# Attention over kept tokens: in the last pair of heads the short chunk goes second, and the output chunks are finished and stored one by one

## The chip, the cores and the metric

The kernel runs on one core of one Trainium2 chip. The metric is device time in microseconds (us). Before the change the median of three runs was 635.94 us (634.38 to 639.89).

## The reference

```
def _L0_cond_ref(x, mask, Wq, Wo):        # x (8, 512, 1024), mask (8, 1024) of 0 and 1
    NH = 8; NEG = -1e+30
    B, D, T = x.shape
    dk = D // NH                          # 64
    scale = 1.0 / sqrt(dk)
    xt = transpose(x, (0, 2, 1))
    q = xt @ Wq.T
    qh = q.reshape(B, T, NH, dk).transpose(0, 2, 1, 3)
    scores = scale * einsum('bhqd,bhkd->bhqk', qh, qh)
    logits = (scores * cmask + (1.0 - cmask) * NEG) * rmask
    attn = softmax(logits, axis=-1)
    ctx = einsum('bhqk,bhkd->bhqd', attn, qh)
    out = ctx.transpose(0, 2, 1, 3).reshape(B, T, D) @ Wo.T
    return transpose(out, (0, 2, 1))
x = x + _L0_cond_ref(x, cond_2048, Wq, Wo)
```

Queries, keys and values are the same projection. The mask (`cmask` over keys, `rmask` over queries) is 1 for about half of the 1024 tokens. A token whose mask is 0 gets the mean over all tokens; the kept tokens attend to kept tokens only.

## The kernel before

The kernel works on the kept tokens alone. For each batch it gathers them into a compact list of NK = 536 places (KH = 268 is half of it), so that the list falls into five chunks of keys and of output rows: four long ones of 128 (`c` or `i` = 0 to 3) and a short one of 24 (`LAST` = 4). Everything is float32. The eight heads of a batch are taken as four pairs (`pr` = 0 to 3), `pairs` lists (batch, pair) in order, and `late` runs over them. There is no scheduler: each engine executes in the order in which the code is written, and `plan` is a table, written by hand, that puts side work (projections, transposes, output products, loads) into slots named (batch, pair, chunk).

In the slot of chunk `c` of a pair:

- `scores(pair, c)`: TensorE (PE) multiplies the queries of the pair with the keys of the chunk into PSUM tiles of tag "s" (two tiles of two banks each; a long chunk uses both, one per head, the short one uses one). ScalarE (ACT) then takes the exponential into `e` (or `el` for the short chunk), one instruction per head, and adds up the sums for the softmax.
- `open_slot` notes what PE has to wait for before it writes with another row tile: the first reader of a "t" bank in the last slot, or else the exponential of head 0 of this slot. `pass_gate` hangs that wait on the first product of `weigh`.
- `weigh_behind(pair, before, c)`: PE multiplies values with `e` of chunks whose exponentials are done (`weigh`, into the two banks `av`). A long chunk is weighed in two halves (`cross` 0 and 1), the short one once.

After a pair, `end_values` copies `av` to `cT`, and `inverses` turns the sums into reciprocals. `spread` sends these through PE (`rb`) to all rows; `contexts` multiplies them into `cT`. For the last pair of all `end_values_last` multiplies `av` with `rb` on VectorE (DVE), first half, then `sum_last`, then second half.

The output of a batch is the product of `cT` of its four pairs with `woT`, one bank of 128 rows by 512 for each long chunk. In the last batch it is made in two steps. `begin_output` adds pairs 0 to 2 in a "t" bank, and ACT copies that to a tile `pa` (tag "xin"). `end_output` multiplies pair 3 in a bank `po`, DVE adds `pa` and writes `oc`, and SP stores `oc` to the DRAM tensor `od`. `plan` puts `begin_output` of the short chunk and of chunks 0 and 1 into slot 3 of the last pair, that of chunk 2 into slot 4; that of chunk 3 stands in `late` behind the last pair.

Then `fetch_last` issues eight indirect DMAs from GpSimd (POOL), which gather for each 128 tokens their rows of `od` into tiles `g`; the first reads the short chunk and chunk 0, the second also chunk 1, the third also chunk 2, the others all. `finish_tokens` transposes each `g` on PE (`o`), adds x on DVE and writes the result from ACT's queue.

Of the kernel before, what the change touches and what calls it, by code (L numbers as in the profile page):

```python
# [10 lines left out]
F32 = mybir.dt.float32  # L11
# [294 lines left out]
def attention_of_kept_tokens(ctx, tc, x, mask, wq, wo, out, ident, wqT, woT, verdict, flag):  # L306
# [360 lines left out]
    def open_slot():  # L667

        gate[0] = reader[0] or reader[1]
        reader[0] = None  # L670
# [52 lines left out]
    def weigh(pair, c, cross):  # L723


        v, e = vs[pair], es[pair, c]
        first = (pair, c) not in begun
        begun.add((pair, c))
        if c == 0 and first:
            avs[pair] = [bank("av_%d_%d_%d" % (*pair, hf), "av") for hf in range(2)]  # L730
        for r in range(2):
            rows = slice(r * DK, (r + 1) * DK)
            hf = r ^ cross
            for h in range(2):
                mm = nc.tensor.matmul(  # L735
                    avs[pair][hf][heads[h], :KH],
                    v[rows, c, heads[h]],
                    e[rows, h, hf, :] if c < LAST else e[rows, h, :],
                    start=(c == 0 and first),
                    stop=(c == LAST),  # L740
                )
                pass_gate(mm)

    def weigh_behind(pair, before, c):


        cross = c in (2, 4)
        if c == 0:
            if before:
                weigh(before, LAST - 1, cross)  # L750
                weigh(before, LAST, cross)
            return
        if c > 1:
            weigh(pair, c - 2, cross)
        weigh(pair, c - 1, cross)
# [16 lines left out]
    def end_values_last(pair):  # L772

        cT = place_contexts(pair)
        for hf, av in enumerate(avs.pop(pair)):
            if hf:
                sum_last(pair)
            cols = slice(hf * KH, (hf + 1) * KH)
            nc.vector.tensor_tensor(cT[:, cols], av[:, :KH], rbs[pair][:, cols], ALU.mult)
        mean_last(pair)  # L780
# [200 lines left out]
    def plain(pr):  # L981
        return woT[:, pr, :].rearrange("p (a d f) -> p d a f", a=A, d=ND)

    def last_products(b, i, prs, po):

        n = max(Q, sizes[i])
        for pr in prs:
            first, last = pr == prs[0], pr == prs[-1]
            if i < LAST:
                to = po.rearrange("p (d a f) -> p d a f", a=A, d=ND)  # L990
                nc.tensor.matmul(  # L991
                    to, cTs[b, pr][:, i * P : i * P + n], plain(pr), start=first, stop=last
                )
                continue
            w = D * n // P
            for j in range(P // n):
                nc.tensor.matmul(
                    po[j * n : (j + 1) * n, :w].rearrange("p (d a f) -> p d a f", a=A, f=Q),
                    cTs[b, pr][:, i * P : i * P + n],
                    plain(pr)[:, j * (w // P) : (j + 1) * (w // P)],  # L1000
                    start=first,
                    stop=last,
                )
# [4 lines left out]
    def begin_output(b, i):  # L1008

        po = bank(f"pa_{b}_{i}")  # L1010
        last_products(b, i, range(ND - 1), po)
        pa = sb.tile([P, D], F32, tag="xin", name=f"pa_{b}_{i}", bufs=NC)
        note(nc.scalar.copy(pa[:, : width(i)], po[:, : width(i)]))
        partials[i] = pa

    def end_output(b, i, tag):
        n, w = max(Q, sizes[i]), width(i)
# [316 lines left out]
    def plan():  # L1334
# [5 lines left out]
        def put(b, pr, c, task, *args, rank=0):  # L1340
            todo[b, pr, c].append((rank, task, args))
# [109 lines left out]
            for i, at in enumerate(ends):  # L1451
                put(*at, finish_blocks, b, i, rank=(2, 2, 2, 6.8, 4.5)[at[2]])

        last = B - 1
        for i in (LAST, 0, 1, 2):
            put(last, 3, 3 + (i == 2), begin_output, last, i, rank=7)
        for k in range(ND):
            put(*((0, 3, 1), (0, 3, 2), (0, 3, 3), (1, 1, 2))[k], mix_weights, k, rank=5.5)
        put(0, 0, 1, turn_mixed, rank=7)
# [9 lines left out]
    def late(n):  # L1469
# [41 lines left out]
        for p, pair in enumerate(pairs):  # L1511
            b, pr = pair
            before = pairs[p - 1] if p else None
            final = p + 1 == len(pairs)
            for c in range(NC):
                scores(pair, c)
                open_slot()
                tasks = sorted(todo[b, pr, c], key=lambda t: t[0])
# [26 lines left out]
        while stores[0] or stores[1]:  # L1545
            issue_stores()
        last = pairs[-1]
        open_slot()
        weigh_behind(None, last, 0)
        spread(last, inverses(last))  # L1550
        begin_output(B - 1, LAST - 1)
        end_values_last(last)
        worst = sb.tile([P, 2], F32, tag="worst", name="worst")
        nc.vector.tensor_reduce(
            worst[:, 0:1], low.rearrange("p h c -> p (h c)"), axis=AX.X, op=ALU.min
        )
        nc.vector.tensor_reduce(worst[:, 1:2], lowest, axis=AX.X, op=ALU.min)
        nc.vector.tensor_tensor(worst[:, 0:1], worst[:, 0:1], worst[:, 1:2], ALU.min)
        for j, i in enumerate((LAST, 0, 1, 2, 3)):
            end_output(B - 1, i, ("t", "av")[j % 2])  # L1560
            if i == LAST:
                pt = ps.tile([P, 2, NB], F32, tag="s", name="worst_t")
                nc.tensor.transpose(pt[:1, 0, :P], worst[:, 0:1], ident)
            elif i == 1:
                one = sb.tile([1, 1], F32, tag="one", name="one")
                nc.vector.tensor_reduce(one, pt[:1, 0, :P], axis=AX.X, op=ALU.min)
                nc.vector.tensor_scalar(one, one, TINY, None, ALU.is_lt)
        nc.vector.tensor_copy(flag, one)
        fetch_last(B - 1)
# [105 lines left out]
```

## Time and profile before

| what | value |
|---|---|
| profiled execution | 637.8 us, span from first to last instruction 635.8 us |
| median of three runs | 635.94 us (634.38 to 639.89) |
| PE busy | 591.4 us (93% of the span) |
| DVE, ACT, POOL busy | 404.7, 348.2, 253.1 us |
| chain that ended last | PE 74%, DMA 9%, DVE 6%, issue 4% |
| HBM | 181 GB/s over the span |

The chain is followed back from the last instruction, at each step to what released it. A name such as `pa L991` gives the tile that is written and the line. A row of the timeline merges like instructions: start, length, engine, line, operation, tiles, shape, count, and in brackets the idle time before it with what ended it. A float32 product on PE shows as two instructions. The profiled execution lay 1.9 us above the median; the work that the change touches lies in its last 55 us.

### The profile page before, as it was taken

How to read it: one execution, taken by the hardware profiler on the slowest of the kernel's cores; microseconds unless marked ns; L12 is line 12 of the kernel's file. 1: busy time of each engine (PE TensorE's matmuls, PEld its weight loads, DVE VectorE, ACT ScalarE, POOL GpSimd, SP SyncE). 2: the span in 40 equal slices, each digit the busy share in tenths (PEclk: the TensorE clock that was granted, in tenths of full speed). 3: DMA queues.
4: the chain of work that ended last, by engine and by line, in shares of the span. 5: the costliest groups of instructions: out<-in, count | busy, mean ns of one | idle time of the engine just before them, and what ended most of it. 6: DMA issues, size and time to landing. Idle time of an engine off the chain costs nothing.

```text
span 635.8 us, 22524 instructions
## 1 busy us (share of the span) xinstructions
PE 591.4 (93%) x9296; PEld 447.1 (70%) x9296; DVE 404.7 (64%) x1191; ACT 348.2 (55%) x986; POOL 253.1 (40%) x363
## 2 busy tenths in 40 slices
PE   6689989999999999999999999999999998898964
PEld 4557756678877787788877877788777876685432
DVE  6546768766575777757875677667765663665343
ACT  5366667666556566566556665567555545435300
POOL 4501333410245525445255534543445525528021
PEclk9799979999999999999999999999999999999985
DMA  8746535432457867886888867886766667788737
GB/s 271 243 129 190 201 99 146 139 117 82 142 174 195 221 134 239 274 221 131 234 252 237 178 149 226 266 228 128 191 196 147 134 164 191 148 268 158 168 121 220
DMA packets 100152, 116.80 MB, mean 184 GB/s; under 512 B 13224, under 2 KB 67048, under 8 KB 100040
## 3 DMA queue, kind: packets, MB, share of 16 engines
q1 hardware_dynamic: 76176, 76.56, 40.9%
q0 software_dynamic: 19520, 36.58, 25.2%
q10 hardware_dynamic: 4344, 2.12, 1.1%
q8 instruction: 75, 1.23, 0.8%
q14 instruction: 37, 0.30, 0.2%
HBM read 72.68 MB, written 42.54 MB: 181 GB/s over the span
## 4 chain that ended last, share of the span: by engine, by line
PE 74%; DMA 9%; DVE 6%; issue 4%; POOL 2%; ACT 2%; SPq 1%; DVEq 0%; POOLq 0%; ACTq 0%
PE av L735 18%; PE s L688 17%; PE pq L554 15%; PE ph L934 12%; PE v L592 3%; PE xc L495 2%; DMA g<-od,origin 2%; PE s L702 2%; DMA od<-joined 2%; PE pa L991 2%; POOL g L1088 1%; DVE joined L958 1%; PE po L878 1%; ACT e L711 1%; DMA x<-in_x_dram 1%
## 5 line engine op out<-in xcount | busy, mean ns | idle before, releaser
L711 ACT ACTIVATE e<-s,bias 128x536 f32<-128x536 f32 x256 | 178.1, 700 | 55.5 <-PE s L688 54.1
L735 PE MATMUL av<-e,v 64*64 64x268 f32 x2048 | 169.2, 392 | 8.4 <-ACT el L711 5.5
L688 PE MATMUL s<-qT 64*64 64x268 f32 x2048 | 168.8, 391 | 0.8 <-issue 0.6
L554 PE MATMUL pq<-xc,wqT 64*64 64x268 f32 (+1 forms) x1984 | 134.8, 388 | 0.1
L735 PEld LDWEIGHTS av<-e,v 64*64 64x64 f32 x2048 | 89.5, 133 | 44.9 <-ACT el L711 8.8
L688 PEld LDWEIGHTS s<-qT 64*64 64x64 f32 x2048 | 100.0, 133 | 24.1 <-ACT e L711 4.4
L554 PEld LDWEIGHTS pq<-xc,wqT 64*64 64x64 f32 x1984 | 97.3, 134 | 20.5 <-DVE m L641 0.8
L826 POOL DMA_DIRECT2D row<-rt x120 | 63.7, 554 | 98.6 <-DVE rt L823 95.7
L1088 POOL DMA_INDIRECT g<-od,origin x48 | 77.4, 1613 | 20.8 <-issue 15.0
L482 POOL DMA_INDIRECT xin<-xd,source x40 | 39.4, 984 | 58.4 <-PE av L735 18.9
L601 DVE COPY v<-v 128x320 f32<-128x320 f32 x64 | 28.4, 486 | 46.2 <-PE v L592 46.2
L711 ACT ACTIVATION_READ_ACCUMULATOR e<-s,bias 128x1 f32 x256 | 50.1, 196 | 0.0
L934 PE MATMUL ph<-wo,mix 128*128 128x256 f32 x168 | 39.5, 383 | 2.3 <-DVE joined L958 2.3
L464 DVE TENSOR_SCALAR_CACHE_REDUCE junk<-rank,key 128x1024 f32<-128x1024 f32 (+4 forms) x40 | 39.9, 997 | 2.6 <-DMA rank<-ranks 2.6
L711 ACT ACTIVATE el<-s,bias 128x268 f32<-128x268 f32 x64 | 30.3, 480 | 19.6 <-PE s L702 19.2
L427 ACT ACTIVATE junka<-x 128x512 f32<-128x512 f32 x64 | 40.2, 628 | 0.7
L958 DVE TENSOR_TENSOR joined<-ph,side 128x512 f32<-128x512 f32 x28 | 19.1, 684 | 32.3 <-PE ph L934 32.3
L1058 DVE STREAM_TRANSPOSE whole<-g 128x512 f32<-128x512 f32 x56 | 36.6, 684 | 4.5 <-DMA g<-od,origin 4.5
L769 ACT COPY cT<-av 128x268 f32<-128x268 f32 x62 | 22.0, 383 | 29.2 <-PE av L735 29.2
L934 PEld LDWEIGHTS ph<-wo,mix 128*128 128x128 f32 x168 | 30.5, 190 | 9.2 <-DVE joined L958 2.7
L975 POOL DMA_DIRECT2D od<-joined x14 | 10.9, 776 | 63.7 <-DVE joined L958 63.5
L401 DVE STREAM_TRANSPOSE xt<-x 128x1024 f32<-128x1024 f32 x28 | 34.2, 1224 | 0.2
(180 smaller groups left out, 816.0 us busy)
## 6 DMA issues: line engine op xcount, KB each, us to landing
xd<-xt SPq DMA_DIRECT2D x120, 128.0 KB
x<-in_x_dram SPq DMA_DIRECT2D x56, 256.0 KB
g<-xd SPq DMA_DIRECT2D x48, 256.0 KB
out_dram<-whole SPq DMA_DIRECT2D x20, 512.0 KB
rb<-row SPq DMA_DIRECT2D x60, 160.0 KB
od<-joined POOLq DMA_DIRECT2D x14, 512.0 KB
out_dram<-whole SPq DMA_DIRECT2D x16, 256.0 KB
rank<-ranks SPq DMA_DIRECT2D x7, 512.0 KB
```

The costliest lines, as they stand in the source:

```text
L401: nc.vector.transpose(xt.rearrange("p k (d f) -> p k d f", d=ND), xs[b][r][:, :, at : at + n].rearrange("p d (k t) -> p k d t", t=Q),)
L427: nc.scalar.activation(junk, xs[b][r][:, d, :], AF.Copy, accum_out=xbars[b][:, d, r : r + 1])
L464: nc.vector.tensor_scalar(junk[:, :n], rank[:, i * P :], key[:, col], 0.0, ALU.is_le, ALU.add, accum_out=found[:, col])
L482: nc.gpsimd.indirect_dma_start(out=xin[:n, :], out_offset=None, in_=rows_of_x[b], in_offset=bass.IndirectOffsetOnAxis(ap=searches[b][2][:n ...
L554: mm = nc.tensor.matmul(pqs[pair][hf][heads[h], :n], wqT[rows, d, at : at + DK], xcs[b][rows, d, hf * KH : hf * KH + n], start=(not cross ...
L688: nc.tensor.matmul(s[h][to, hf, :KH], qT[heads[h], at : at + DK], qT[heads[h], hf * KH : (hf + 1) * KH], start=True, stop=True,)
L711: act = nc.scalar.activation(e[:, h], of[h], AF.Exp, bias=biases[pair][:, c : c + 1], scale=SCALE, accum_out=acc[:, h, c : c + 1],)
L735: mm = nc.tensor.matmul(avs[pair][hf][heads[h], :KH], v[rows, c, heads[h]], e[rows, h, hf, :] if c < LAST else e[rows, h, :], start=(c == ...
L826: nc.gpsimd.dma_start(row[:, :, a, :].rearrange("h c j -> (h c) j"), rt[a * Q : a * Q + 2 * NC, :])
L934: nc.tensor.matmul(po[:, t * m : (t + 1) * m], left[:, i, t * P : (t + 1) * P], right[:, i, :], start=(i == 0), stop=(i == 1),)
L1058: nc.vector.transpose(whole.rearrange("p (d a) n -> p a d n", a=A)[:, :, :, i * Q : (i + 1) * Q], gs.pop((b, i)).rearrange("p (a d f) -> p ...
L1088: nc.gpsimd.indirect_dma_start(out=gs[b, i], out_offset=None, in_=ods[b], in_offset=bass.IndirectOffsetOnAxis(ap=origin[:, b, i : i + 1] i ...
```

## The change

1. In the last pair of the last batch the chunks are taken in the order 0, short, 1, 2, 3. `weigh_behind` has an order of its own for this pair.
2. `begin_output` of the long chunks goes out of `plan`. Each long chunk now gets the products of all four pairs in one bank: chunks 0 and 1 in the two "s" tiles, opened behind the last slot, with their pairs 0 to 2 between the last weighing and `rb`; chunks 2 and 3 whole, behind the others. Only the short chunk keeps its partial sum.
3. ACT copies a finished bank to `oc` (`store_output`), where DVE added `pa`; SP stores it at once. The order of finishing is 0, short, 1, 2, 3 (before: short, 0, 1, 2, 3).

```
@@ weigh
-                    stop=(c == LAST),
+                    stop=bool(not cross and c == LAST - 1) if pair == pairs[-1] else c == LAST,
@@ weigh_behind
+        if c and pair == pairs[-1]:
+            for k in {LAST: (0,), 1: (0,), 2: (LAST, 1), 3: (1, 2)}[c]:
+                weigh(pair, k, c in (1, 3))
+            return
@@ last_products
-    def last_products(b, i, prs, po):
+    def last_products(b, i, prs, po, starts=True, ends=True):
...
-            first, last = pr == prs[0], pr == prs[-1]
+            first, last = starts and pr == prs[0], ends and pr == prs[-1]
@@ new functions
+    def open_output(b, i):
+        return ps.tile([P, 2, NB], F32, tag="s", name=f"po_{b}_{i}")[:, 0, :]
+
+    def store_output(b, i, po):
+        oc = sb.tile([P, D], F32, tag="oc", name=f"oc_{b}_{i}", bufs=ND)
+        nc.scalar.copy(oc, po)
+        nc.sync.dma_start(place_outputs(b)[places[i], :], oc)
@@ plan
-        last = B - 1
-        for i in (LAST, 0, 1, 2):
-            put(last, 3, 3 + (i == 2), begin_output, last, i, rank=7)
@@ late
-            for c in range(NC):
+            for c in (0, LAST, 1, 2, 3) if final else range(NC):
...
         last = pairs[-1]
+        first, second = (open_output(B - 1, i) for i in range(2))
+        last_products(B - 1, 0, range(2), first, ends=False)
+        weigh(last, LAST - 1, 1)
+        inv = inverses(last)
+        begin_output(B - 1, LAST)
+        last_products(B - 1, 0, [2], first, starts=False, ends=False)
         open_slot()
-        weigh_behind(None, last, 0)
-        spread(last, inverses(last))
-        begin_output(B - 1, LAST - 1)
+        for k in (LAST - 2, LAST - 1):
+            weigh(last, k, 0)
+        spread(last, inv)
+        last_products(B - 1, 1, range(ND - 1), second, ends=False)
         end_values_last(last)
+        last_products(B - 1, 0, [ND - 1], first, starts=False)
+        store_output(B - 1, 0, first)
+        end_output(B - 1, LAST, "t")
+        last_products(B - 1, 1, [ND - 1], second, starts=False)
+        store_output(B - 1, 1, second)
         worst = sb.tile([P, 2], F32, tag="worst", name="worst")
...
-        for j, i in enumerate((LAST, 0, 1, 2, 3)):
-            end_output(B - 1, i, ("t", "av")[j % 2])
-            if i == LAST:
...
+        for i in range(2, LAST):
+            po = open_output(B - 1, i)
+            last_products(B - 1, i, range(ND), po)
+            store_output(B - 1, i, po)
+            if i == 2:
...
```

Three places show how the instructions move. In the names the batch is left out; `s_3_4` are the scores of pair 3, chunk 4, `e_3_0` the exponentials of chunk 0.

PE at the head of the last pair, after its scores of chunk 0 and the last weighing of pair 2, before:

```order
L688 MATMUL s_3_1_0_8783<-qT_3_8536 64x268 x2
L688 MATMUL s_3_1_1_8784<-qT_3_8536 64x268 x2
L688 MATMUL s_3_1_0_8783<-qT_3_8536 64x268 x2
L688 MATMUL s_3_1_1_8784<-qT_3_8536 64x268 x2
L735 MATMUL av_3_0_8795<-e_3_0_8748,v_3_8651 64x268 x2
L735 MATMUL av_3_1_8796<-e_3_0_8748,v_3_8651 64x268 x2
L794 MATMUL rb_0_8803<-ident,ris_88 64x128 x8
L794 MATMUL rb_4_8813<-ident,ris_88 64x128 x2
```

and now:

```order
L702 MATMUL s_3_4_8783<-qT_3_8536 64x268 x4
L735 MATMUL av_3_0_8790<-e_3_0_8748,v_3_8651 64x268 x2
L735 MATMUL av_3_1_8791<-e_3_0_8748,v_3_8651 64x268 x2
L688 MATMUL s_3_1_0_8797<-qT_3_8536 64x268 x2
L688 MATMUL s_3_1_1_8798<-qT_3_8536 64x268 x2
L688 MATMUL s_3_1_0_8797<-qT_3_8536 64x268 x2
L688 MATMUL s_3_1_1_8798<-qT_3_8536 64x268 x2
L735 MATMUL av_3_1_8791<-e_3_0_8748,v_3_8651 64x268 x2
L735 MATMUL av_3_0_8790<-e_3_0_8748,v_3_8651 64x268 x2
L798 MATMUL rb_0_8815<-ident,ris_88 64x128 x8
L798 MATMUL rb_4_8825<-ident,ris_88 64x128 x2
```

The short chunk's scores and both halves of chunk 0's weighing now stand ahead of `rb` of pair 2.

PE from the last weighing to the last output product, before (`rb` here is the last pair's):

```order
L735 MATMUL av_3_0_8795<-el_3_4_8898,v_3_8651 64x268 x2
L735 MATMUL av_3_1_8796<-el_3_4_8898,v_3_8651 64x268 x2
L794 MATMUL rb_0_8942<-ident,ris_89 64x128 x8
L794 MATMUL rb_4_8952<-ident,ris_89 64x128 x2
L991 MATMUL pa_3_8956<-woT,cT_0_8252 128x512 x2
L991 MATMUL pa_3_8956<-woT,cT_1_8769 128x512
L997 MATMUL po_4_8974<-woT,cT_1_8769 32x128 x4
L1563 MATMUL worst_t<-ident,worst 1x128
L991 MATMUL po_0_8987<-woT,cT_1_8769 128x512
L991 MATMUL po_1_8992<-woT,cT_1_8769 128x512
L991 MATMUL po_2_9000<-woT,cT_1_8769 128x512
L991 MATMUL po_3_9005<-woT,cT_1_8769 128x512
```

and now:

```order
L798 MATMUL rb_0_8929<-ident,ris_89 64x128 x8
L798 MATMUL rb_4_8939<-ident,ris_89 64x128 x2
L995 MATMUL po_1_8892<-woT,cT_0_8252 128x512 x2
L995 MATMUL po_1_8892<-woT,cT_1_8769 128x512
L995 MATMUL po_0_8891<-woT,cT_1_8769 128x512
L1001 MATMUL po_4_8958<-woT,cT_1_8769 32x128 x4
L995 MATMUL po_1_8892<-woT,cT_1_8769 128x512
L995 MATMUL po_2_8977<-woT,cT_0_8252 128x512 x2
L995 MATMUL po_2_8977<-woT,cT_1_8769 128x512 x2
L1586 MATMUL worst_t<-ident,worst 1x128
L995 MATMUL po_3_8990<-woT,cT_0_8252 128x512 x2
L995 MATMUL po_3_8990<-woT,cT_1_8769 128x512 x2
```

Behind `rb` stood seven long products and stand thirteen; chunks 0 and 1 are finished among the first of them, chunks 2 and 3 as the last eight.

ACT in the same stretch, before:

```order
L1013 COPY pa_4_8884<-pa_4_8871 128x128
L1013 COPY pa_0_8890<-pa_0_8886 128x512
L1013 COPY pa_1_8896<-pa_1_8892 128x512
L711 ACTIVATE el_3_4_8898,sums_87<-s_3_4_8899,bias_3_8736 128x268 x2
L1013 COPY pa_2_8918<-pa_2_8914 128x512
L801 COPY rb_3_8941<-rb_0_8942 128x512
L801 COPY rb_3_8941<-rb_4_8952 128x128
L1013 COPY pa_3_8960<-pa_3_8956 128x512
L1028 DMA od_8973<-oc_4_8979 24x128 x2
```

and now:

```order
L1017 COPY pa_4_8917<-pa_4_8904 128x128
L805 COPY rb_3_8928<-rb_0_8929 128x512
L805 COPY rb_3_8928<-rb_4_8939 128x128
L1025 COPY oc_0_8954<-po_0_8891 128x512
L1040 DMA od_8956<-oc_4_8963 24x128 x2
L1025 COPY oc_1_8970<-po_1_8892 128x512
L1025 COPY oc_2_8982<-po_2_8977 128x512
L1025 COPY oc_3_8995<-po_3_8990 128x512
```

The copies of the partial sums of the long chunks are gone, those of the finished chunks stand behind `rb`, and the store issues of the short chunk stand between the first two of them.

More of the change, by code (lines that the diff above doesn't have):

```diff
@@ L1558, in late @@
         nc.vector.tensor_tensor(worst[:, 0:1], worst[:, 0:1], worst[:, 1:2], ALU.min)
-        for j, i in enumerate((LAST, 0, 1, 2, 3)):
-            end_output(B - 1, i, ("t", "av")[j % 2])
-            if i == LAST:
-                pt = ps.tile([P, 2, NB], F32, tag="s", name="worst_t")
-                nc.tensor.transpose(pt[:1, 0, :P], worst[:, 0:1], ident)
-            elif i == 1:
+        for i in range(2, LAST):
[3 more added lines that the diff above has]
+            if i == 2:
+                pt = bank("worst_t")
+                nc.tensor.transpose(pt[:1, :P], worst[:, 0:1], ident)
                 one = sb.tile([1, 1], F32, tag="one", name="one")
-                nc.vector.tensor_reduce(one, pt[:1, 0, :P], axis=AX.X, op=ALU.min)
+                nc.vector.tensor_reduce(one, pt[:1, :P], axis=AX.X, op=ALU.min)
                 nc.vector.tensor_scalar(one, one, TINY, None, ALU.is_lt)
```

## The prediction

> **What bounds the kernel now.** I read the chain of waits first, since the change touches only the last pair of the last batch. Its end, in columns start, length, what:
>
> ```profile
> 609.73 3.45 PE po L991 x8
> ...
> 613.27 0.69 DVE oc L1023
> 613.99 2.00 DMA od<-oc
> ...
> 616.77 0.95 POOL g L1079
> ...
> 623.03 5.47 DMA g<-od,origin
> ...
> 628.64 1.10 PE o L1105 x4
> ...
> 629.77 0.69 DVE x L1106
> ```
>
> TensorE (PE) finishes the four long output chunks at 613.18, the last is added (0.69) and stored (2.00, landing at 615.99), eight gathers on GpSimd read the stored rows back, and each is transposed, added to x and sent out. From the eighth gather's landing (623.03 + 5.47 = 628.5) to the end of the span (635.8) are 7.3 us. The timelines of GpSimd, the SP queue and PE tell what starts the gathers:
>
> ```profile
> 611.35 0.34 SPq L1025 DMA_DIRECT2D od<-oc  x1
> ...
> 614.18 1.00 POOL L1079 DMA_INDIRECT g<-od,origin  x1 [25.78 <-DVE flag L1568]
> ...
> 618.03 0.95 POOL L1079 DMA_INDIRECT g<-od,origin  x1 [0.30 <-issue]
> ...
> 623.03 0.95 POOL L1079 DMA_INDIRECT g<-od,origin  x1 [0.30 <-issue]
> ...
> 617.77 2.33 PE L1105 MATMUL o<-ident,g 128*128 128x128 f32 x8 [4.60 <-DMA g<-od,origin]
> ```
>
> The first gather needs the short chunk and chunk 0. Chunk 0's store is issued at 611.35; with the 2.00 us of the last store it lands near 613.4, and the gather starts 0.8 later. (The page names the flag, but the gather needs no flag; in the chain, too, 616.77 follows a landing at 615.99 by 0.78.) From there on GpSimd gives a gather every 1.26 us ((623.03 - 614.18)/7). The fourth gather, the first that needs chunk 3, could start at 615.99 + 0.78 = 616.77, but its turn comes at 618.03: the queue of gathers, not the last chunk, bounds it. Landings are slower: 617.77 for the first, 628.5 for the eighth, 1.53 us apart, and 3.6 us after issue for the first, 5.5 for the last. Last, by stages (PE, PEld, DVE, ACT, POOL busy; granted clock; DMA share; GB/s):
>
> ```profile
> 582.00:593.00 11.00, 9.33 (x140) 5.06 (x132) 9.18 (x25) 6.75 (x20) 5.50 (x4) 1.00 0.93 149
> ...
> 602.00:609.00 7.00, 5.86 (x44) 2.64 (x42) 2.41 (x10) 1.34 (x3) 0.00 (x0) 1.00 0.00 0
> ...
> 614.00:624.00 10.00, 4.84 (x18) 3.33 (x19) 2.77 (x5) 0.00 (x0) 7.66 (x8) 0.60 0.82 254
> 624.00:636.00 12.00, 3.91 (x16) 2.39 (x14) 2.76 (x4) 0.00 (x0) 0.00 (x0) 0.50 0.65 190
> ```
>
> The DMA engines stand still from 602 to 609, and then carry all the last batch's output at once.
>
> **The change, part by part.** *Short chunk second.* PE's early slots:
>
> ```profile
> 585.58 1.31 PE L794 MATMUL rb<-ident,ris 128*64 128x128 f32 x20 [0.97 <-DVE ris L814]
> ...
> 588.90 1.81 PE L688 MATMUL s<-qT 64*64 64x268 f32 x16
> 591.25 1.13 PE L735 MATMUL av<-e,v 64*64 64x268 f32 x16 [0.54 <-ACT e L711]
> 592.32 0.86 PE L997 MATMUL pa<-woT,cT 128*32 128x128 f32 x24
> ```
>
> and ScalarE's (ACT) instructions that matter:
>
> ```profile
> 582.88 0.66 ACT L769 COPY cT<-av 128x268 f32<-128x268 f32 x2
> 583.85 0.71 ACT L711 ACTIVATE e<-s,bias 128x536 f32<-128x536 f32 x1 [0.31 <-PE s L688]
> ...
> 599.21 0.48 ACT L711 ACTIVATE el<-s,bias 128x268 f32<-128x268 f32 x1
> ...
> 600.05 0.20 ACT L711 ACTIVATION_READ_ACCUMULATOR el<-s,bias 128x1 f32 x1
> ```
>
> The short chunk's exponentials (599.21 to 600.25, 1.04 us) move in between the cT copies, which end at 583.54, and chunk 1's, now at 583.85. Chunk 1's scores need the bank that the short chunk's exponentials read, so PE completes them some 0.7 us after 584.6, and chunk 1's first exponential moves from 583.85 to about 585.4. The weighing behind it waits for that one (0.9 us, as at 591.25), so rb goes from 585.58 to about 586.8. All later slots keep their distances: the last ends at 593.5 instead of 592.3, 1.2 later. But the short chunk's scores and weighing are then done; they took
>
> ```profile
> 598.46 0.68 PE L702 MATMUL s<-qT 64*64 64x268 f32 x8
> 598.96 1.08 PE L735 MATMUL av<-e,v 64*64 64x268 f32 x16
> ...
> 603.49 0.68 PE L735 MATMUL av<-e,v 64*64 64x268 f32 x8 [0.68 <-ACT pa L1013]
> 603.99 0.63 PE L735 MATMUL av<-el,v 64*64 64x268 f32 x8
> 604.55 1.31 PE L794 MATMUL rb<-ident,ris 128*64 128x128 f32 x20
> 606.33 2.84 PE L991 MATMUL pa<-woT,cT 128*128 128x512 f32 x6 [0.47 <-ACT rb L801]
> ```
>
> 0.50 (598.46 to 598.96) and 0.56 (603.99 to 604.55). Net **+0.15**; bounds 0 (the delay fully used) and +1.2 (none of it).
>
> *Waits that go.* In the rows above PE stood 0.68 for ACT's copy of pa 2 and 0.47 for its rb copy, since the next PE work used a bank of the same pair. Now only the short chunk has a partial sum to copy, ahead of which PE has chunk 0's third pair to do, and behind rb comes chunk 1 in a bank of its own: **-1.15** (bound 0, if other copies take their place).
>
> *A wait that comes.* Chunk 0's fourth pair needs cT of the last pair:
>
> ```profile
> 602.85 0.58 ACT L1013 COPY pa<-pa 128x512 f32<-128x512 f32 x1 [2.61 <-PE pa L991]
> 605.70 0.75 ACT L801 COPY rb<-rb 128x512 f32<-128x512 f32 x2 [2.26 <-PE rb L794]
> ...
> 606.31 0.44 DVE L779 TENSOR_TENSOR cT<-av,rb 128x268 f32<-128x268 f32 x1 [5.19 <-ACT rb L801]
> ...
> 608.53 0.17 DVE L785 COPY cT<-qm 128x9 f32<-128x9 f32 x1
> ...
> 609.92 0.97 ACTq L1028 DMA_DIRECT2D od<-oc  x2
> ```
>
> The first half of cT is ready 0.9 us after PE's rb ends (605.86), all of it 2.84 after (608.70). Three pairs of chunk 1 fill 2.84 of PE. So PE waits 0 to 0.3: **+0.1**. Behind it stand all of PE's remaining products.
>
> PE thus ends at 613.18 + 0.15 - 1.15 + 0.1 = 612.3. No product is added or dropped: sixteen long ones stay sixteen.
>
> *The stores.* ACT's copy (0.58, row 602.85) takes the place of the vector engine's (DVE's) addition (0.69): **-0.1** ahead of chunk 3's store, which is issued at 613.0 and lands at 615.0. The earlier chunks: at 0.86 a product (3.45/4), PE ends chunk 0 near 603.3, the short one at 603.7, chunk 1 at 604.5, chunk 2 at 608.2. ACT's two store issues for the short chunk (0.97) now stand ahead of its copy of chunk 1 and delay it by some 0.6; PE doesn't need that bank before chunk 3, at 608.4, so it costs nothing, and would cost the 0.6 if chunk 1 were last. On SP chunk 0's store moves ahead of the short chunk's; nothing else stands there. With 2.0 for a store and 0.8 for the release, gathers 0, 1 and 2 start near 607, 608.5 and 611.7, and gather 3 at 615.0 + 0.8 = 615.8 instead of 618.0: **-2.2**. The bound at work changes from the queue of gathers to the last chunk. Their buffers no longer wait for five partial sums, which were read before 613.97 anyway: nothing.
>
> *The tail.* Gathers 3 to 7 follow 1.26 apart by issue but landed 1.53 apart. Gather 3 lands 3.6 after its issue (the first gather's time, as the queue is empty again), gather 7 four landings later: 615.8 + 3.6 + 6.1 = 625.5, against 628.5: **-0.8** beside the 2.2. From there to the end 7.3 stay, less what the outputs of chunks 0 to 2 of the tokens, now gone before the rush, leave free. These are eight such transfers:
>
> ```profile
> out_dram<-x ACTq DMA_DIRECT2D x8, 256.0 KB
> ```
>
> The last one's own path doesn't shorten; three fewer queue ahead of the rush. Each is 256 KB, 1.0 us at the 254 GB/s of 614 to 624. Bounds 0 and -2; I take **-0.5**, near 0, because the last transfer is issued only after its own gather.
>
> Sum: PE and the copy bring chunk 3's store from 613.99 to 613.0; as gather 3 no longer stands in a queue, that makes 2.2 at gather 3, and 0.8 and 0.5 follow in the tail: **-3.5**. The profiled execution took 637.8 (span 635.8), so 634.3; it lay 1.9 above the median of the runs, 635.94. Taken off that median: **632.4**.
>
> The Trainium skill ("DMA: Bandwidth & Descriptors", Issuing engines are not separate DMA queues) says that transfers from all issuing engines share the same 16 DMA engines and interleave. The 0.00 DMA share from 602 to 609 says that the first stores meet nothing; later ones could, and by the rule alone the early gathers would be paid back in part, the second rival's result.
>
> **The rivals.** *The tail moves together with its rate (-5.5, 630.4).* If the DMA rate and not the release bounds gathers and outputs, what leaves before 615.8 (three gathers and two to three outputs of 256 KB, at 254 GB/s 5 to 6 us of transfer) comes off the end. For it: 254 GB/s from 614 to 624 against 190 after. Against: gather 3's start is PE's affair, and after it come 5.0 of issue, 3.6 of landing and, of the 7.3, all but the 1.4 that a last transfer in empty queues might save, 630.3 of span: a floor, met only if nothing queues.
>
> *The early traffic delays the last store (-1.4, 634.5).* Gather 2 and the first output move while chunk 3 is stored; two transfers of 256 KB take 2.1 us at 254 GB/s, and if they go first, gather 3 is 2.1 later. For it: 0.82 DMA share there. Against: four stores in a row each landed in 2.0.
>
> *Slower: the clock is halved in the last pair (+3.3, 639.2).* The new waits stand at the head of the last pair. PE was idle 1.7 of 11 us there (row 582 to 593); it would be about 2.9. Twice a stretch that was not full was followed by the half clock:
>
> ```profile
> 76.77:83.60 6.83, 5.62 (x101) 4.14 (x94) 4.73 (x9) 5.16 (x14) 2.92 (x17) 1.00 0.56 188
> 83.60:90.42 6.82, 6.14 (x62) 3.09 (x63) 3.04 (x11) 3.88 (x14) 0.00 (x0) 0.50 0.40 110
> ...
> 612.66:616.07 3.41, 0.51 (x2) 0.00 (x0) 1.22 (x3) 0.00 (x0) 1.58 (x2) 1.00 0.72 263
> ```
>
> A stretch of 6.83 us full of work at half clock costs 3.4. One eats the gain; from the second on the change loses: 6.8 - 3.5 = +3.3. For it: 5.62 busy of 6.83 sufficed at 76.77. Against: the slots at 582 to 593 have waits already, at clock 1.00. The Trainium skill ("TensorE: Matmul & The Clock Gate", Part 1: The HAM clock gate) has the clock fall after an idle window of about 3.4 us. The fall at 616 agrees (0.51 busy in the 3.41 before); the one at 83.6 came after far more work. By that rule alone waits below 1 us never bring it.
>
> That the change doesn't do what it says I exclude: the order of SP and PE shows each chunk stored before the next but one is begun.
>
> **How the numbers follow.** Forecast 0.64 (own range 630.9 to 633.9: one of PE's terms at its bound makes gather 3 about 1.1 to 1.5 later with the tail's, the tail at its bound takes 1.5 more off); rate-bound tail 0.15; delayed store 0.12; half clock 0.09. The range reaches from the rate-bound tail, with half a microsecond for the runs' spread, to one halved stretch (632.4 + 3.4): 629.9 to 635.9. About what a measurement of this kernel can tell from no change is 1%, 6.4 us. Faster by that needs 629.6, the far end of the first rival: 0.12. Slower by that, 642.3, needs three halved stretches or a wait that I don't see: 0.05. Within: 0.83.
>
> **What would show it.** Right: gather 0 near 607, gather 3 near 615.8 released by the store of chunk 3, PE's last product ending near 612.3, idle of PE below 0.3 between rb and that product, DMA share above 0 between 604 and 609. Wrong: gather 3 at 617 or later; chunk 3's store taking over 2.5 us; the half clock before 610; a wait of PE for DVE's cT above 0.5; or gather 7 landing over 11 us after gather 3's start.

## The result, and the profile after

The changed kernel took 633.57 us (median of 18 runs, 631.13 to 638.06) beside 636.32 for the kernel before on the same chip (18 runs, 633.39 to 641.61); ratio 0.9949, 95% interval 0.9928 to 0.9971. The forecast was 632.4 and "within 1%". The profiled execution took 632.02 us, its span 630.1.

Of the 5.7 us between the two spans (635.8 and 630.1) only a part belongs to the change. The last instruction that both kernels share unmoved is the second exponential of chunk 0 in the last pair. In ACT's timeline of the kernel before:

```profile
582.20 0.69 ACT L711 ACTIVATE e<-s,bias 128x536 f32<-128x536 f32 x1
```

and of the changed kernel:

```profile
578.56 0.70 ACT L711 ACTIVATE e<-s,bias 128x536 f32<-128x536 f32 x1
```

So 3.64 us were there already, in work that is the same in both. All comparisons below count from this instruction, called the mark. From it to the end of the span the kernel before took 53.60 (635.8 - 582.20), the changed one 51.54: 2.06 less.

**PE.** Its timeline after the change, at the head of the last pair and at the end of its products:

```profile
579.95 0.68 PE L735 MATMUL av<-e,v 64*64 64x268 f32 x8 [0.56 <-ACT cT L773]
...
582.56 0.68 PE L735 MATMUL av<-e,v 64*64 64x268 f32 x8 [0.54 <-ACT e L711]
583.17 1.31 PE L798 MATMUL rb<-ident,ris 128*64 128x128 f32 x20
...
588.84 1.13 PE L735 MATMUL av<-e,v 64*64 64x268 f32 x16 [0.54 <-ACT e L711]
...
600.22 0.43 PE L1001 MATMUL po<-woT,cT 128*32 128x128 f32 x8
600.58 4.56 PE L995 MATMUL po<-woT,cT 128*128 128x512 f32 x10
...
605.08 3.60 PE L995 MATMUL po<-woT,cT 128*128 128x512 f32 x8
```

rb of the pair ahead starts 4.61 after the mark (before: 585.58, 3.38), 1.23 later, as the short chunk's work stands ahead of it. The last product ends at 608.68, 30.12 after the mark (before: 613.17, 30.97): 0.85 earlier. From 582 to 609 the list of PE's waits (sum, times, longest) has one entry, the exponentials, once ahead of this rb and once behind it; the waits of 0.68 and 0.47 for copies are gone:

```profile
PE av L735 <- ACT e L711: 1.1, 2, 0.5
```

Before, PE's waits from the mark to the last product were 0.97, 0.54, 0.68 and 0.47, together 2.66; now 0.56, 0.54 and 0.54, together 1.64.

**The chain of waits**, columns start, length, what:

```profile
605.24 3.45 PE po L995 x8
...
608.72 0.59 ACT oc L1025
...
609.33 2.10 DMA od<-oc
...
612.19 0.94 POOL g L1091
...
615.94 6.07 DMA g<-od,origin
```

and GpSimd's (POOL) timeline with what released each gather:

```profile
604.62 1.00 POOL L1091 DMA_INDIRECT g<-od,origin  x1 [19.49 <-DMA od<-oc]
605.93 0.98 POOL L1091 DMA_INDIRECT g<-od,origin  x1 [0.30 <-issue]
609.53 0.95 POOL L1091 DMA_INDIRECT g<-od,origin  x1 [2.62 <-PE o L1117]
612.19 0.94 POOL L1091 DMA_INDIRECT g<-od,origin  x1 [1.71 <-DVE x L1118]
...
617.20 0.95 POOL L1091 DMA_INDIRECT g<-od,origin  x1 [0.30 <-issue]
```

Gathers 0 to 2 have left the rush (the gathers and outputs that crowd together from gather 3 on). GpSimd is idle for 1.71 ahead of gather 3, which starts 0.76 after chunk 3's store has landed (609.33 + 2.10 = 611.43): the last chunk bounds it now, no longer the queue of gathers. (The timeline names DVE's `x`; the chain shows the store.) It starts 33.63 after the mark, before 35.83 (618.03 - 582.20): 2.20 earlier.

**The tail.** PE and DVE of the changed kernel behind gather 3:

```profile
616.36 2.03 PE L1117 MATMUL o<-ident,g 128*128 128x128 f32 x8 [1.46 <-DMA g<-od,origin]
```

```profile
624.13 0.69 DVE L1118 TENSOR_TENSOR x<-o,x 128x512 f32<-128x512 f32 x1 [0.16 <-PE o L1117]
```

Gather 3's rows are transposed 4.17 after its start (616.36 - 612.19). From its start to the end of the last addition are 12.63 us (624.82 - 612.19); before, 12.43 (630.46 - 618.03). From there to the end of the span 5.28, before 5.34. Here nothing was gained. The stages (PE, PEld, DVE, ACT, POOL busy; granted clock; DMA share; GB/s):

```profile
602.00:609.00 7.00, 7.00 (x21) 3.13 (x19) 0.56 (x3) 1.46 (x3) 1.98 (x2) 1.00 0.52 164
...
614.00:624.00 10.00, 5.87 (x24) 4.22 (x23) 3.46 (x5) 0.00 (x0) 3.23 (x4) 0.50 0.86 237
```

The DMA engines carry 164 GB/s where they stood still before, and PE is not idle for a moment from 602 to 609.

### The profile page after: what moved, and what is told of

Read it like the earlier page. It is cut to its first block, busy times and chain, and to the rows that moved or that the text cites. A ratio compares the mean times of both kernels' runs of the same rounds, so it can differ in the third digit from the quotient of the medians.

```text
span 630.1 us, 22515 instructions
## 1 busy us (share of the span) xinstructions
PE 590.1 (94%) x9296; PEld 446.9 (71%) x9296; DVE 401.7 (64%) x1187; ACT 348.7 (55%) x986; POOL 253.4 (40%) x363
## 3 DMA queue, kind: packets, MB, share of 16 engines
q8 instruction: 75, 1.23, 0.8%
## 4 chain that ended last, share of the span: by engine, by line
PE 74%; DMA 9%; issue 4%; DVE 4%; POOL 3%; SPq 2%; ACT 2%; POOLq 0%; DVEq 0%; ACTq 0%
PE av L735 18%; PE s L688 16%; PE pq L554 15%; PE ph L938 12%; DMA g<-od,origin 3%; PE v L592 3%; POOL g L1100 3%; PE xc L495 3%; PE po L995 2%; DMA od<-joined 2%; PE s L702 2%; DVE joined L962 1%; ACT e L711 1%; DMA out_dram<-whole 1%; DMA x<-in_x_dram 1%
```

## The experiments

All positions are counted from the mark of the run itself, in us; they come from the timelines of each run's profile. "PE end" is the end of the last output product, "behind" the stretch from gather 3's start to the end of the span.

| kernel | PE end | gather 2 | gather 3 | behind | mark to end |
|---|---|---|---|---|---|
| before | 30.97 | 34.57 | 35.83 | 17.77 | 53.60 |
| changed | 30.12 | 30.97 | 33.63 | 17.91 | 51.54 |
| changed, second profile | 30.12 | 30.95 | 33.61 | 18.63 | 52.24 |
| changed, third profile | 30.39 | 31.50 | 33.87 | 18.18 | 52.05 |
| order alone | 31.30 | 34.98 | 36.24 | 17.68 | 53.92 |
| outputs alone | 30.57 | 31.40 | 34.07 | 17.20 | 51.27 |
| all gathers wait for all rows | 30.13 | 36.14 | 37.40 | 17.72 | 55.12 |
| no outputs 0 to 2 | 30.12 | 30.94 | 33.53 | 16.61 | 50.14 |
| last output alone | 30.12 | 31.10 | 33.52 | 15.89 | 49.41 |
| PE's waits filled twice | 30.44 | 30.48 | 35.91 | 17.28 | 53.19 |
| last chunk in halves | 30.86 | 31.24 | 33.81 | 17.42 | 51.23 |
| PE's wait filled with chunk 2 | 29.71 | 29.99 | 35.00 | 17.49 | 52.49 |
| third output later | 30.12 | 31.06 | 33.60 | 17.49 | 51.09 |

Each row is one profile. PE's positions repeat within 0.01 to 0.27 between profiles of one kernel, the stretch behind gather 3 only within 0.7. The changed kernel's three profiles give -2.06, -1.36 and -1.55 against the one of before, -1.7 on average.

### The changed kernel again

No edit.

> The changed kernel itself, as the yardstick beside the three others. The stretch from the second exponential of chunk 0 of the last pair to the end of the span was 53.6 us before (582.20 to 635.8) and 51.5 in the first profile after (578.56 to 630.1), so 2.1 of the difference of the two spans lie there. Forecast: ratio to before 0.9945 (-3.5 us), stretch 50 to 52 us. If the tail's terms of the prediction (0.8 and 0.5) were real and only missed in one profile, the stretch is near 50.1; if only the release counts, near 51.4.

Measured: 641.01 us beside 641.27, ratio 0.9986 (0.995 to 1.0022), on a chip that was slower for both. Gather 3 stands where it stood, the stretch behind it is 18.63. Both the ratio and the end, at 52.24, miss what was expected (0.9945, and 50 to 52). The chain names the landing that ended last:

```profile
619.53 2.08 DMA od<-oc
...
626.13 6.54 DMA g<-od,origin
```

The size of the gain hangs on this stretch. PE's part and the store's repeat.

### The order alone, the outputs alone

The order alone: `begin_output` goes back into slot 3, the rest as before, with the short chunk second.

```
+        for i in (LAST, 0, 1):
+            put(last, 3, 3, begin_output, last, i, rank=7)
...
+        begin_output(B - 1, 2)
...
-            store_output(B - 1, i, po)
+        for j, i in enumerate((LAST, 0, 1, 2, 3)):
+            end_output(B - 1, i, ("t", "av")[j % 2])
```

> Only the order of the chunks (short second) is taken over; the long chunks keep their partial sums of pairs 0 to 2, copied by ACT, and the addition on DVE, all four finished together at the end. Release theory (the queue of eight gathers, started by chunk 0's store, is what counts): PE ends 0.5 to 1 us earlier relative to the start of the last pair, the first gather goes with it, all gathers stay in one queue: stretch 52.6 to 53.1, -0.5 to -1.0 us against before. Rival (the order alone makes the gain, since it takes PE's waits away): -2 to -3.5 us.

Measured: 642.49 beside 641.27, ratio 1.0033 (1.0002 to 1.0065). PE ends 0.33 later than before, little more than the 0.27 by which profiles of one kernel differ. Its timeline:

```profile
614.60 1.13 PE L735 MATMUL av<-e,v 64*64 64x268 f32 x16 [0.68 <-ACT pa L1017]
...
617.44 2.84 PE L995 MATMUL pa<-woT,cT 128*128 128x512 f32 x6 [0.47 <-ACT rb L805]
```

Both waits for ACT stay, at the very lengths of before. At the head of the pair the wait of 0.97 ahead of rb is gone, but two others, of 0.56 and 0.54, stand in its place, as in the changed kernel. In sum PE waits 2.79 from the mark to its last product, before 2.66. The order alone brings nothing, or a small loss, where 0.5 to 1.0 was expected.

The outputs alone: the changed kernel without the new order.

```
-            for c in (0, LAST, 1, 2, 3) if final else range(NC):
+            for c in range(NC):
```

> Only the outputs chunk by chunk are taken over; the short chunk stays last in the last pair. Release theory: PE now has nothing to do in the last two slots while ACT takes the exponentials of chunk 3 and of the short chunk, so it waits about 1 to 1.5 us there, loses the two old waits of 0.68 and 0.47, and ends about where it did before; the third gather onward is released by chunk 3 and no longer queued: stretch 52 to 52.8, -0.8 to -1.6 us. Rival (early stores and gathers alone make the gain): -2 to -3.5 us, as the whole change.

Measured: 639.66 beside 641.27, ratio 0.9967 (0.9939 to 0.9996). PE ends 0.40 earlier than before, gather 3 starts 1.76 earlier, and the mark to the end is as short as in the whole change. PE's and POOL's timelines:

```profile
596.67 1.14 PE L735 MATMUL av<-e,v 64*64 64x268 f32 x16 [0.69 <-ACT el L711]
```

```profile
616.73 0.95 POOL L1087 DMA_INDIRECT g<-od,origin  x1 [2.72 <-PE o L1113]
619.40 0.95 POOL L1087 DMA_INDIRECT g<-od,origin  x1 [1.72 <-DVE x L1114]
```

The wait of 0.69 is new. Before, the weighing in that slot followed the scores without a wait (598.46, 598.96), since `open_slot` named the read of a partial sum, long done; with the partial sums gone it names the short chunk's own exponential, and nothing stands between. In sum PE waits 2.21 here (0.98, 0.54 and 0.69), in the changed kernel, where the short chunk is second, 1.64. So the parts don't add: +0.33 alone, -0.40 alone, -0.85 together. The order is worth 0.45 of PE with the outputs and nothing that can be seen without them; the gain of the kernel comes with the chunk-by-chunk stores. In the profile the end comes 2.33 earlier than before, as the rival had it; in the medians it is 1.6, the upper end of the theory. Nor do whole runs on this chip show that the order adds anything: 0.9967 for the outputs alone, 0.9986 for both, with intervals that overlap.

### All gathers wait for all rows

```
-            rows = min(NK, END + (i + 1) * P)
+            rows = NK
```

> The changed kernel, but each of the eight gathers waits for the stores of all chunks. Release theory: gather 0 starts where gather 3 starts now, so gather 3 comes three turns (3.8 us) later, and so do the last gather and the end: stretch 55 to 55.5, +3.5 to +4 us against the changed kernel, slightly slower than before. Rival (the tail is bound by the DMA rate and the transfers that go early save their transfer time): three gathers and two outputs of 256 KB at 254 GB/s come back, 5 us. Second rival (the last transfers are bound by something else, and early gathers save nothing): within 1 us of the changed kernel.

Measured: 644.75 beside 641.27, ratio 1.0041 (1.0007 to 1.0076). POOL:

```profile
618.23 1.00 POOL L1091 DMA_INDIRECT g<-od,origin  x1 [27.57 <-DMA od<-oc]
...
622.08 0.94 POOL L1091 DMA_INDIRECT g<-od,origin  x1 [0.30 <-issue]
```

Gather 0 starts with the last store, gather 3 three issues later (3.85), 3.77 after where the changed kernel has it, and the end comes 2.9 to 3.6 later than in the changed kernel's profiles. The medians on this chip, 644.75 and 641.01, say 3.7. Thus the early stores bring nothing here unless the early gathers leave with them, and then about what the issue of three gathers takes.

### Which transfers hold the tail up

Two kernels leave stores of the last batch's results out: the one those of tokens 0 to 383, the other all but the last 128 tokens'.

```
+        if i >= 3:          (the other: i >= 7)
             nc.scalar.dma_start(
                 out[b, :, i * P : (i + 1) * P].rearrange("(d p) t -> p d t", d=ND), xr
             )
```

> The changed kernel without the output transfers of the first three token tiles of the last batch (3 of 8, 256 KB each, left out). In all kernels so far the stretch from gather 3's start to the end of the span was 17.2 to 18.6 us, before the change as after, although three gathers and up to three outputs go earlier after it. If those outputs still queue ahead of the last gathers and outputs (rate): 1 to 2 us shorter, 16 to 17. If the stretch is a chain of issue, landing and one last output that they don't touch: unchanged, 17.2 to 18.6.

> The changed kernel with only the last of the eight output transfers of the last batch (seven left out). It shows the gathers by themselves. If the outputs delay the gathers' landings: the jump of about 3 us before the sixth or seventh landing goes, gather 7 lands 3.5 to 4 us after its issue instead of 5.5, and the last output lands in 2.2 to 2.7 instead of 3.2: the stretch from gather 3 to the end falls to 14.5 to 15.5. If the gathers are slow by themselves: the landings stay as they are, stretch 17 or more.

Measured, one profile each: 632.29 and 633.74 us beside 639.54. Of the first kernel, POOL's timeline with its span, and the chain:

```profile
core 0 of [0], span 630.2 us
...
613.59 0.94 POOL L1091 DMA_INDIRECT g<-od,origin  x1 [1.64 <-DVE x L1118]
```

```profile
618.58 4.11 DMA g<-od,origin
```

and of the second:

```profile
core 0 of [0], span 631.8 us
...
615.91 0.95 POOL L1091 DMA_INDIRECT g<-od,origin  x1 [1.47 <-DVE x L1118]
```

Gather 3 starts where it does in the changed kernel, but without outputs 0 to 2 the rest takes 16.6 (630.2 - 613.59), without outputs 0 to 6 15.9. The complete kernel needs 17.9 to 18.6. Three early outputs, which the prediction took to be gone, cost 1.3 to 2.0 of it. The four others seem to cost 0.7 more, but by that much the stretch also varies from profile to profile.

### The third output later

```
+        if b == B - 1 and i == 2:
+            held.append(store)
+            return
+        store()
+        if b == B - 1 and i == 5:
+            held[0]()
```

> The changed kernel with one store moved: the output of tokens 256 to 383 (the third) is issued behind that of the sixth instead of ahead of the fourth's, so that it doesn't run beside the gathers 3 to 7. Theory (outputs in the rush of gathers hold the landings up): gather 7 lands 0.4 to 0.9 earlier than in the changed kernel (its landing 5.5 after its issue there), and the end comes 0.2 to 0.6 earlier, since the transfer has to be carried later, when the queues have room (0.65 share). Rival (the tail is bound by bytes): the end stays within 0.2 of the changed kernel's or is later by up to 1.0, the 256 KB at 254 GB/s.

> The changed kernel once more, on the same chip as the two others, as their measure: 0.993 to 0.9995 of the kernel before; gather 3 at 33.6 and the end at 51.5 to 52.2 us after the second exponential of chunk 0 of the last pair.

Measured: 632.85 and, for the changed kernel beside it, 632.79 (before on the same chip 637.48); ratios 0.9941 (0.9913 to 0.997) and 0.9943 (0.9911 to 0.9975). The chain with output 2 held back, and that of the changed kernel:

```profile
609.17 2.07 DMA od<-oc
...
617.03 4.54 DMA g<-od,origin
```

```profile
611.59 2.08 DMA od<-oc
...
618.17 5.82 DMA g<-od,origin
```

With output 2 out of the way gather 7 lands at 621.57, 9.56 after gather 3's start (612.01). In the changed kernel gather 6, one ahead of it, lands only then (618.17 + 5.82 = 623.99, 9.57 after 614.42). So the landings are held up by output 2, which is sent into the rush. But the time is the same: its 256 KB are carried later, at the end, and whether that alone takes the gain back no run shows. The profile's end is 0.4 to 1.2 earlier than the changed kernel's three, the medians show none of it. Half of each theory holds.

### PE's waits filled

Both waits of 0.54 for exponentials could hold products. The first try puts pairs 0 and 1 of chunk 2 into the slot of chunk 1, and those of chunk 1 into the slot of chunk 3; ACT copies each to a partial sum, DVE adds it at the end.

```
+                if final and c in (1, 3):
+                    early_part(b, {1: 2, 3: 1}[c])
                 weigh_behind(pair, before, c)
...
-        last_products(B - 1, 1, range(ND - 1), second, ends=False)
+        last_products(B - 1, 1, [2], second, ends=False)
```

> The changed kernel, with the products of pairs 0 and 1 of chunks 2 and 1 moved into the slots of chunks 1 and 3 of the last pair, where PE waits 0.54 us for an exponential before it weighs (two products of 0.86 each fill more than the wait). ACT copies the partial sum, DVE adds it at the end; chunk 3 stays as it is. If these two waits are simply PE time lost ahead of gather 3: PE ends 1.0 to 1.1 earlier (29.1 instead of 30.1 from the second exponential of chunk 0) and gather 3 starts as much earlier, at 32.5 to 32.6. If ACT's two copies delay the exponentials or rb: less than 0.5.

Measured in one profile: 639.37 us beside 639.54. PE, POOL and the chain:

```profile
607.80 0.43 PE L1001 MATMUL po<-woT,cT 128*32 128x128 f32 x8 [0.92 <-DVE cT L789]
```

```profile
614.59 0.95 POOL L1103 DMA_INDIRECT g<-od,origin  x1 [0.78 <-DMA od<-oc]
620.02 0.94 POOL L1103 DMA_INDIRECT g<-od,origin  x1 [4.48 <-DMA od<-oc]
```

```profile
615.19 4.07 DMA od<-oc
```

PE ends 0.32 later than in the changed kernel, where 1.0 to 1.1 earlier was expected. Two things went wrong. The cover behind rb was spent, that is chunk 1's three pairs, behind which the changed kernel hides the making of cT: PE stood 0.92 for it. And chunk 3's store took 4.07 instead of 2.10, behind gather 2, which had started 0.60 ahead of it.

The second try spares the cover: it fills the slot of chunk 3 alone, with chunk 2.

```
+                if final and c == 3:
+                    early_part(b, 2)
                 weigh_behind(pair, before, c)
```

> The changed kernel with one more move: the products of pairs 0 and 1 of output chunk 2 stand in the slot of chunk 3 (last slot of the last pair), where PE waits for an exponential, ScalarE copies them to a partial sum, and VectorE adds it at the end; the cover behind rb stays as in the changed kernel. Theory (the last chunk's store bounds gather 3): PE's last product ends 0.3 to 0.6 earlier (29.5 to 29.8 us after the second exponential of chunk 0 of the last pair, against 30.12), gather 3 starts 33.0 to 33.3 after it (33.63), gather 2 some 1.7 earlier (near 29.3). The third output then leaves before the rush, so that from gather 3 to the end it takes 16.9 to 17.5 (17.9 in the changed kernel): the end 0.7 to 1.5 earlier than the changed kernel's. Rival (the early traffic delays the last store, as where all waits were filled): chunk 3's store takes 3 us or more, gather 3 starts after 34, and the end is not earlier.

Measured: 633.86 beside 632.79 for the changed kernel and 637.48 for that before; ratio 0.9975 (0.9945 to 1.0004). PE, SP and POOL:

```profile
603.72 3.60 PE L995 MATMUL po<-woT,cT 128*128 128x512 f32 x8
```

```profile
607.97 0.32 SPq L1038 DMA_DIRECT2D od<-oc  x1
```

```profile
607.60 0.95 POOL L1103 DMA_INDIRECT g<-od,origin  x1 [0.30 <-PE po L995]
612.61 0.95 POOL L1103 DMA_INDIRECT g<-od,origin  x1 [4.05 <-DMA od<-oc]
```

PE ends at 607.32, 29.71 after the mark and 0.41 earlier than in the changed kernel, as the theory had it. But gather 3 starts 4.64 after the issue of chunk 3's store (607.97 to 612.61), in the changed kernel 2.86 (609.33 to 612.19). With the same 0.76 for the release the store took 3.9. Gather 2 had started 0.37 ahead of it; in the changed kernel it starts 0.20 behind. The rival won: PE's 0.41 were turned into a loss of 1.4 at gather 3.

### The last chunk in two halves

Chunk 3 is multiplied in two halves of 256 columns, each copied and stored by itself.

```
@@ output_by_halves, in place of store_output for chunk 3
+        for h in range(2):
+            to = po[:, h, :n].rearrange("p (d a f) -> p d a f", a=A, d=ND // 2)
+            for pr in range(ND):
+                nc.tensor.matmul(to, cTs[b, pr][:, i * P : (i + 1) * P], ...)
+            cols = slice(h * n, (h + 1) * n)
+            nc.scalar.copy(oc[:, cols], po[:, h, :n])
+            nc.sync.dma_start(...)
```

> The changed kernel, with chunk 3's four products made in two halves of 256 columns in two banks; each half is copied by ACT and stored (128 KB) when it is complete. PE time should stay (a half product takes 0.43), the copy ahead of the last store falls from 0.59 to about 0.33, and the last store carries 128 KB instead of 256. If a store's 2.1 us are mostly latency: gather 3 0.25 to 0.4 earlier; if they follow the bytes: 0.6 to 1.0 earlier.

Measured in one profile: 634.89 us beside 639.54. PE, and the last store in the chain:

```profile
608.48 1.89 PE L1027 MATMUL po<-woT,cT 128*128 128x256 f32 x8
610.84 1.99 PE L1027 MATMUL po<-woT,cT 128*128 128x256 f32 x8 [0.46 <-ACT oc L1035]
```

```profile
613.27 1.69 DMA od<-oc
```

Half the bytes make the store only 0.4 shorter, so the larger part of its 2.10 does not go with the bytes. Its copy is 0.2 shorter (0.38 in the chain), but PE ends 0.74 later: 0.46 is the wait for the copy of the first half, whose bank lies in one tile with the second's, and the two halves take 1.74 and 2.01 in the chain, 0.3 more than the 3.45 of the whole. Gather 3 starts 0.2 later. In this form nothing is gained.

## Why the prediction was right, and by which steps

The forecast of 632.4 and the measured 633.57 lie 1.2 apart, and the mechanism is the one it gave. By its own steps:

- **Short chunk second, +0.15; waits that go, -1.15; the wait for cT, +0.1.** Together -0.9, measured -0.85. The slots end 1.23 later (1.2 forecast), both waits are gone, and the wait for cT is nil: the short chunk's products (600.22) follow the others without a gap. The step that looked separable was not: of the outputs' -1.15 only 0.40 shows without the new order, since the wait of 0.69 for the short chunk's exponentials comes up in place of those removed. The sum held because both halves were made.
- **Copy and store.** Chunk 3's store is issued 30.77 after the mark (609.33), before 31.79 (613.99 - 582.20): 1.02 earlier, forecast 1.0. It takes 2.10, forecast 2.0.
- **Gather 3, -2.2.** Measured -2.20, released by the store, as forecast. This is the heart of the gain, and the kernel in which all gathers wait for all rows loses it with 2.9 to 3.6 us.
- **Gathers 0 to 2.** They start 26.06, 27.37 and 30.97 after the mark; forecast were 607, 608.5 and 611.7 on the scale of before, which is 24.8, 26.3 and 29.5. They are 1.1 to 1.5 late: chunk 0's copy ends at 600.92, and gather 0, which needs the short chunk's stores too, issued up to 602.1, starts 3.7 later, not 2.8; and chunk 2's store, issued at 605.8 among gathers 0 and 1, took some 3.0 (609.53 less 0.76). This delays gather 2 and with it output 2.
- **The tail's landings, -0.8, and its outputs, -0.5.** These terms failed. Gather 3 to the end of the last addition took 12.63 where 11.6 was forecast, and from there to the end it stayed at 5.3. The step at fault is the sentence that outputs 0 to 2 are gone before the rush. They are not: outputs are issued from 609.9 on, and output 2's addition ends at 615.63 by DVE's timeline, between the starts of gathers 5 and 6. Without outputs 0 to 2 the stretch behind gather 3 is 16.6, nearly the 16.5 that the two terms gave (17.8 less 1.3); with them it is 17.9 to 18.6. So for a queue without these outputs the sum of the two terms came out, but by luck: there the last landing (618.58 + 4.11 = 622.69) comes 9.1 after gather 3, where 9.7 was forecast, and 7.5 follow, where 6.8 was forecast. (The landings that the forecast reckoned from were read from PE's start, 617.77 for the first; with the 0.14 from a landing to PE's start that one came near 617.63, which changes little.)

Gather 3's 2.2 less the 0.1 to 0.9 that the tail lost leaves 1.4 to 2.1 in the profiles. The runs' medians differ by 2.75, and the three measurements of the ratio, 0.9949, 0.9986 and 0.9943, agree with 2 within their intervals. Whether the gain is nearer 1.5 or 3 stays open: the first 580 us, which are the same in both kernels, spread by more. The forecast's own range, 630.9 to 633.9, was wide enough to hold the result although the tail's 1.3 did not come.

Of the rivals, the **rate-bound tail** (-5.5) is refuted: the DMA engines carried 164 GB/s from 602 to 609 and the end moved by 2. The **delayed last store** did not come in the changed kernel (2.10), where gather 2 starts 0.20 behind the store: it came, with 1.8 to 2.0 us, in both kernels that brought gather 2 ahead of the store, by 0.37 and 0.60. (With the last chunk in halves gather 2 starts 0.06 ahead of the last half's store, 613.21 to 613.27, and this store still takes only 1.69.) Chunk 2's store, among gathers 0 and 1, shows a smaller delay (3.0) in the changed kernel itself. The Trainium skill ("DMA: Bandwidth & Descriptors", Issuing engines are not separate DMA queues) has all transfers interleave on the same 16 engines; output 2 in the rush, which holds the landings up, agrees with it. The **half clock** did not come: from 576 to 609 the granted clock is 1.00, with PE waiting three times 0.54 to 0.56. Nor did PE's idle time at the head of the pair grow to the 2.9 us that this rival reckoned with: of the 11 us from 578 to 589 PE is busy for 9.22.

## What to carry to other kernels

When a chain passes through PE, a store and a queue of gathers, first find which of them holds the next step: 0.85 us of PE gave 2.2 us at the gather, because the early gathers left the queue at the same time. An edit that empties a queue early pays only as far as what it sends early is finished by the time of the rush; price its followers (here the outputs) too. And the two parts of an edit can each uncover the wait that the other removes, so a sum over parts measured apart (+0.33 and -0.40) would have missed nearly all of PE's gain.

## What the runs showed of the hardware

Chunk 3's store of 256 KB to DRAM took 1.99 to 2.10 us alone or with a gather starting 0.2 to 0.5 us behind it, but 4.07 with a gather started 0.60 ahead of it and 3.9 with one started 0.37 ahead. That the order of two starts a few tenths apart is worth 2 us was not expected. The landings and the packets show more. Gather 2 of the kernel with chunk 2 filled in, in its chain:

```profile
607.60 4.18 DMA g<-od,origin
```

It lands at 611.78, and chunk 3's store near 611.85 (gather 3's start at 612.61 less 0.76). With the waits filled twice PE's timeline has

```profile
619.19 0.98 PE L1129 MATMUL o<-ident,g 128*128 128x128 f32 x4 [1.88 <-DMA g<-od,origin]
```

and with 0.14 from a landing to PE's start (611.78 to 611.92 in the other) gather 2 landed near 619.05; the store landed at 619.26. Both times the store's end is seen 0.1 to 0.2 after that of the gather started ahead of it. In the changed kernel gather 2 starts behind the store, and the store, landing at 611.43, doesn't wait for it: PE has its rows from 613.82 on. The Trainium skill ("DMA: Bandwidth & Descriptors", Queues, rings and completion order) says that the increment which reports a transfer's end lands only after every earlier write of the same DMA engine, across its queues. These four times agree with that, but the rule isn't what made these stores late, as the packets on the DMA queues show (queue, packets, MB, share; q1 carries SP's stores here, q0 the gathers). The changed kernel from 610.0 to 611.1:

```profile
q1 hardware_dynamic: 144, 0.26, 69.0%
```

The whole store, 144 packets, moves in this time, with none of a gather beside it. The kernel with chunk 2 filled in, from 610.0 to 611.0:

```profile
q0 software_dynamic: 55, 0.20, 60.4%
q1 hardware_dynamic: 25, 0.04, 10.8%
```

Here 25 of the store's 144 packets still move beside the gather's 55, and 13 more follow until 611.5. So the store's own data came late, and not only the report of its end. It lands near 611.85, 0.35 after its last packet; in the changed kernel it lands at 611.43, 0.35 after 611.08. With the waits filled twice, too, eight of its packets move only from 618.2 on, the last until 618.9, and it lands at 619.26. So nothing is left for a wait on the gather's writes: the transfers shared the DMA engines, as the rival of the delayed store had it. A part of the delay may belong to gather 1, whose packets still move when the store begins (from 608.7 to 609.3 q0 has 40 beside the store's 36); no run took the two gathers apart.
